# Four moves in a hybrid attention and long-convolution kernel: sample loads, filter negatives, branch matrices, tail stores

## The chip, the cores and the metric

The kernel runs on one core of one Trainium2 chip. A core has five engines that run their own instruction streams in order: TensorE (PE, matmuls and transposes), VectorE (DVE), ScalarE (ACT), GpSimd (POOL) and SyncE (SP, which here only issues transfers). Transfers (DMAs) between the device memory and the on-chip memory are issued by SP, ACT or POOL and carried out by 16 shared DMA engines. The metric is device time in microseconds of one execution; less is better.

## The reference, cut to what matters

Two images of 128 channels and 64x64 positions go through two layers. The first is a windowed attention block with small linear layers. The second flattens each image to 4096 tokens of 128 channels and does a full attention without projections (with a masked diagonal), and then a spectral filter bank: 16 long causal filters `phi`, applied to the sequence and to its sign-alternated copy, mixed by 2x16 matrices of 128x128, plus three short lags. Of four candidate branches one set of weights is formed by a softmax and an argmax.

```python
x = x + conv_block(group_norm(x))                      # layer 0: 7x7 window attention + three linears
t = to_tokens(x)                                       # (2, 4096, 128)
a = layer_norm(t)
sim = a @ a.T / sqrt(128); sim[diagonal] = -1e9
t = t + softmax(sim) @ a                               # layer 1: full attention
u = layer_norm(t)
for i, frac in enumerate((1, 2, 4, 8)):                # layer 1: filters, four branches
    ui = u[:, : T // frac]
    U_plus  = causal_conv(phi, ui)                     # 16 filters
    U_minus = sgn * causal_conv(phi, sgn * ui)
    out_i = einsum(U_plus, sigma**.25, M_plus[i]) + einsum(U_minus, sigma**.25, M_minus[i]) \
          + sum(shift(ui, lag) @ M_u[i][lag] for lag in range(3))
w = one_hot(argmax(y)) - y + y                         # y = softmax(log_weights + gumbel)
out = from_tokens(t + sum(w[i] * pad(out_i)))
```

## The kernel before, in words

All work is float32 on one core. The convolution is done as a transform in blocks: the tokens of each image are transformed by matmuls with a table `tr` into 160 bins (the tensor `us` in device memory), the filters `phi` into the same bins (the tensor `gs`), and the last stage reads both back block by block.

**Stages.** (1) Layer 0 runs in bands of eight image rows through a list of small pieces, written out by hand with due times (`PLAN`); the order on PE, DVE, ACT and POOL is fixed by that list. (2) `attention(0, fill)` runs the full attention of image 0. It goes over pairs (a, c) of eight chunks of 512 tokens; each step makes one score tile (L938), its exponential on ACT (L943) and one product for the keys (L1068). The same weights are needed turned around for the other chunk: four exponential tiles are sent to device memory by ACT (`eb`, L970), read back two steps later by SP into `et` (L977, two buffers), turned in blocks of 32 by DVE at the seventh step (L986), and multiplied by PE from the eighth step on (L996). PE's order is recorded, so if `et` is late PE stands still. (3) `attention(1, fill)` does the same for image 1. (4) A tail finishes the last chunks. (5) The last stage multiplies block by block: `burst` (L1596, copied to `y` at L1601) and `project` (L1615).

**Fillers.** At each step both attentions call `fill()`. It sends waiting stores, and then takes one piece from generators: the `urgent` list (`after`, which divides by the softmax sums, normalises, transforms a finished chunk of 512 tokens into bins and stores them to `us`; and `short_lags`), then the list `steps`. In attention 0 `steps` is: `drain()` (left over pieces of layer 0), `chosen = branch_weights()`, `filters()`, `tokens(1, bank)`. In attention 1 a third list, `slow`, holds `for_ffn()`: it loads the branch matrices (`st`, L1306, 32 loads of 256 KB by POOL), mixes them on DVE (L1328 to L1337) and scales them on ACT (L1342), and last loads the first four blocks for the last stage. It is stepped at every second step: `if turns_[0] % 2: next(slow, None)`. In attention 1 `steps` begins with what attention 0 left in `urgent`.

**Small loads and the POOL queue.** `branch_weights` loads `lw`, `gu` and `sg` on SP (L1253 to L1255); its second piece raises `sg` to a power on POOL (L1259). The filter samples are loaded into `zc` by four DMAs on SP (L906), each of 128x32 runs of eight values (32 bytes); in the built program they stand ahead of the load of `sg`. On POOL, L1259 stands ahead of the pieces that normalise the last chunk of image 0 (`k.pw`, L714 and L715, and `k.z`, L720), which PE transposes next (L202).

**Filters.** `filters()` reads `zc`, transforms it (L1375), accumulates four partial sums in `places` (a region of the tile `cm[1]`), and for each makes sums and differences on POOL (`fb`, L1388) and, for the imaginary parts, the negatives on DVE (`fn`, L1401 and L1402). `fb`, `fn` and the `ub` of `after` (L1169) share one ring of four buffers, tag "ub".

**Stores.** `fresh` puts a store into a list; `stores()` sends it two steps later, on POOL (L1103); `room()` sends more when over three buffers are listed. A ring buffer is free again only when its store has landed. In the tail the sums `ub` are made by DVE, and the stores still go through the list to POOL. The tiles of the last stage (`y` among them) take over memory that the ring has held, so the first copy to `y` waits for the last of the tail's stores.

Of the kernel before, what the change touches and what calls it, by code (L numbers as in the profile page):

```python
# [8 lines left out]
F32 = mybir.dt.float32  # L9
# [5 lines left out]
P = 128  # L15
# [6 lines left out]
KF = 16  # L22
# [80 lines left out]
def kernel(  # L103
# [773 lines left out]
    with ap_:  # L877
# [20 lines left out]

        zc = [tp.tile([P, 2, TH + 1], F32, name="zc"), tt0.rearrange("p (s t) -> p s t", s=2)]
        nc.gpsimd.memset(zc[0][:, :, 0:1], 0.0)  # L900
        pns = {}
        for hh in range(SG // 2):
            for e in range(2):
                at = 1 + (2 * hh + e) * 2 * LG * KF
                pns[hh, e] = zc[0][:, 0, at : at + 2 * LG * KF].rearrange("p (k l f) -> p k l f", k=KF, l=2)
                nc.sync.dma_start(  # L906
                    out=pns[hh, e].rearrange("p k l f -> p (k l) f"),
                    in_=bass.AP(
                        phi_pad.tensor, P - FB + (2 * P * hh + e) * FB, [[2 * FB, P], [PHW, 2 * KF], [1, LG]]
                    ),  # L910
                )

        def attention(b, fill):


# [199 lines left out]
            turns_[1] += 1  # L1115

        def fresh(to, part, by=nc.gpsimd):
            queued_.append((turns_[0], turns_[1], by, to, part))

        def stores_left():  # L1120
            while queued_:
                send_one()


        def after(b, c):

            yield True
            n0 = 4 * c
            par, hf = divmod(c, 4)
            hh, fp = divmod(hf, NFP)  # L1130
            pt = bank()
            for j in range(4):
                nc.tensor.transpose(pt[:, j * P : (j + 1) * P], xa[b][:, (n0 + j) * P : (n0 + j + 1) * P], ident)
            rden = sp.tile([P, 4], F32, tag="rden", name="rden")
            kept_, out_ = tt[b][:, n0 : n0 + 4, :], pt.rearrange("p (j d) -> p j d", d=P)
            nc.vector.reciprocal(rden, out_[:, :, P - 1])
            rest = sp.tile([P, 4], F32, tag="rest", name="rest")
            nc.vector.tensor_reduce(rest, out_[:, :, 0 : P - 1], AX.X, ALU.add)
            for j in range(4):
                nc.vector.scalar_tensor_tensor(  # L1140
                    kept_[:, j, 0 : P - 1], out_[:, j, 0 : P - 1], rden[:, j : j + 1], kept_[:, j, 0 : P - 1],
                    ALU.mult, ALU.add,
                )
            nc.vector.tensor_tensor(rest, rest, rden, ALU.mult)
            nc.vector.tensor_tensor(kept_[:, :, P - 1], kept_[:, :, P - 1], rest, ALU.subtract)
            yield
            z = sp.tile([P, 4, P], F32, tag="z4", name="z4")
            stats = ln_statistics(kept_)
            yield
            yield True  # L1150
            ln_apply(z, kept_, stats)
            yield
            yield True
            pt = bank()
            transposed(pt, z)
            s0 = 1 + 2 * P * hh * FB
            to = zc[b][:, par, s0 : s0 + 2 * P * FB].rearrange("p (c e f) -> p e f c", e=2, f=FB)
            nc.scalar.copy(to[:, :, 2 * fp : 2 * fp + 2], pt.rearrange("p (e f c) -> p e f c", e=2, f=2))
            yield

            def store(pu, n, r0, m, ri):

                for s in range(2):
                    both = sp.tile([P, 512], F32, tag="uo", name="uo", bufs=2)
                    nc.scalar.copy(both[:, 0 : 2 * n], pu[s][:, 0 : 2 * n])  # L1165
                    room()
                    ub = sp.tile([P, 2, 256], F32, tag="ub", name="ub", bufs=4)
                    for sgn, op in enumerate((ALU.add, ALU.subtract)):
                        adder[0].tensor_tensor(ub[:, sgn, 0:n], both[:, 0:n], both[:, n : 2 * n], op)  # L1169
                    to = us[b, par, r0 : r0 + m, :, :, 2 * hh + s, 2 * fp : 2 * fp + 2]  # L1170
                    if ri is not None:
                        fresh(to[:, :, ri].rearrange("k g f d -> k g (f d)"), ub)
                        continue
                    for sgn in range(2):
                        for f in range(2):
                            fresh(to[:, sgn, :, f].rearrange("k i d -> i k d"), ub[64 * f : 64 * f + 64, sgn, 0:P])

            for r0, c0 in row_tiles:
                for ri in range(2):
                    pu = [bank() for _ in range(2)]  # L1180
                    for e in range(2):
                        for s in range(2):
                            rows_ = slice(s * 64, (s + 1) * 64)
                            nc.tensor.matmul(  # L1184
                                pu[s][:, e * 256 : (e + 1) * 256], lhsT=tr[rows_, hh, e, c0 + ri * P : c0 + (ri + 1) * P],
                                rhs=z[rows_, 2 * e : 2 * e + 2, :].rearrange("p f d -> p (f d)"), start=True, stop=True,
                            )
                    store(pu, 256, r0, P, ri)
                    yield
                    if len(crowd_[0]) < 2:  # L1190
                        yield True

            pu = [bank() for _ in range(2)]
            for e in range(2):
                for f in range(2):
                    for s in range(2):
                        rows_ = slice(s * 64, (s + 1) * 64)
                        nc.tensor.matmul(
                            pu[s][f * 64 : (f + 1) * 64, e * P : (e + 1) * P], lhsT=tr[rows_, hh, e, left_col:],
                            rhs=z[rows_, 2 * e + f, :], start=True, stop=True,  # L1200
                        )
            store(pu, P, left_row, 32, None)
            yield
            if len(crowd_[0]) < 2:
                yield True


# [137 lines left out]

        def filters():

            ph = {}
            for (hh, e), pn in pns.items():
                at = (2 * hh + e) * LL  # L1350
# [15 lines left out]
            for r0, c0, parts_, m in everything:  # L1366
                places = cm[1][:, SG * LL : (3 * SG) * LL].rearrange("p (j e c) -> p j e c", j=SG, e=2)
                for j in range(SG):
# [26 lines left out]
                            store(fb[mine], r0, n, ri, s, 1, 1)  # L1395
                    if 1 in parts_:
                        mine = slice(m - n, m)
                        room()
                        fn = sp.tile([P, 2, LL], F32, tag="ub", name="fn", bufs=4)
                        one, two = sums[mine, 0, :], sums[mine, 1, :]  # L1400
                        nc.vector.scalar_tensor_tensor(fn[mine, 0, :], one, -1.0, two, ALU.mult, ALU.subtract)  # L1401
                        nc.vector.tensor_tensor(fn[mine, 1, :], two, one, ALU.subtract)  # L1402
                        store(fn[mine], r0, n, 1, s, 1, 0)
# [8 lines left out]
        def filler(b, steps, kept, slow=()):  # L1412

            urgent, done = [], []
            slow = iter(slow)
            crowd_[0] = urgent

            def fill(c=None):
                if c is not None:
                    done.append(c)  # L1420
                    urgent.append(after(b, c))
                    if len(done) % 4 == 0:
                        lags = short_lags(b, len(done) // 4 - 1)
                        if kept is not None:
                            kept.append(lags)
                            lags = residual_of(lags)
                        urgent.append(lags)
                    return

                stores()  # L1430
                if turns_[0] % 2:
                    next(slow, None)
                for queue in (urgent, steps):
                    while queue:
                        got = next(queue[0], False)
                        if got is None:
                            return
                        if got:
                            break
                        queue.pop(0)  # L1440
                if kept and len(done) == 7:
                    next(kept[0], None)

            return fill, urgent
# [14 lines left out]

        chosen = branch_weights()  # L1460
        next(chosen)
        steps = [drain(), chosen, filters(), tokens(1, bank)]

        kept = []
# [69 lines left out]
        fill, left = filler(1, steps, kept, slow)  # L1534
        attention(1, fill)
        adder[:] = [nc.vector]
        crowd_[0] = [None, None]
        for gen in (*steps, slow):
            for _ in gen:
                pass  # L1540
# [3 lines left out]
        while chains:  # L1544
            for gen in chains[:2]:
                if next(gen, 0) == 0:
                    chains.remove(gen)
                stores()
            next(kept[0], None)
            next(held, None)  # L1550
        stores_left()
        for _ in residuals:
            next(kept[0], None)
            next(held, None)
# [332 lines left out]
```

## Time and profile before

| | us |
|---|---|
| median of three runs (1998.31 to 1998.85) | 1998.82 |
| the profiled execution, its own time | 1999.0 |
| its span in the profile | 1997.2 |
| PE busy | 1906.4 (95%) |
| DVE, ACT, POOL busy | 951.8, 733.0, 749.4 |
| layer 0, and its hand-over to attention 0 | 0 to about 347 |
| attention 0 | about 347 to 767 |
| attention 1 | about 767 to 1172 |
| tail | 1172 to about 1239 |
| last stage | about 1239 to 1997 |

A line of the timeline gives the start, the duration, the engine, the line of the kernel, the operation and how many of it were merged; in square brackets stands the idle time of the engine ahead of it and what ended that. A line of the waits gives the waiting engine and line, what it waited for, and the total, the number and the longest of these waits in microseconds. A line of the table of windows gives the stretch, its length, the busy time of PE, of PE's weight loads, of DVE, ACT and POOL (each with its number of instructions), the granted clock of PE as a share of full speed, the busy share of the DMA engines and GB/s.

### The profile page before, as it was taken

To read this page: it belongs to the slowest core of one execution; us is meant where nothing else is said; L and a number is where in the kernel's file an instruction comes from. 1 tells how busy PE (TensorE), PEld (TensorE's weight loads), DVE (VectorE), ACT (ScalarE), POOL (GpSimd) and SP (SyncE) were. 2 spreads that over 40 slices of the span, in tenths; PEclk is the share of its full clock that TensorE was granted. 3 is DMA by queue.
4 is the path that set the end of the run, shared out by engine and by line. 5 is a ranking of instruction groups with operands and counts; after the bars stand their busy time and mean duration, and the time that the engine had idled before them with its cause. 6 is when DMAs were issued, how large, how long until landed. Compare 5 with 4: busy or idle time off the path is not lost.

```text
span 1997.2 us, 50806 instructions
## 1 busy us (share of the span) xinstructions
PE 1906.4 (95%) x20504; PEld 1350.6 (68%) x20504; DVE 951.8 (48%) x2934; ACT 733.0 (37%) x1718; POOL 749.4 (38%) x1227
## 2 busy tenths in 40 slices
PE   6899998899899999999999998999999999999998
PEld 4677776344344444444444445999998999999987
DVE  5799997354445534454433464333333343333332
ACT  3788986322133333232322313222222222222221
POOL 4366886334542346434332343222222212222211
PEclk8999999899899999999999999999999999999999
DMA  4222222567575543888676413222222223222211
GB/s 156 61 61 59 62 60 49 133 180 221 175 222 163 159 139 116 234 227 249 186 196 192 137 48 86 68 68 66 68 67 54 54 73 85 67 66 69 66 43 44
DMA packets 248185, 226.20 MB, mean 113 GB/s; under 512 B 128495, under 2 KB 202239, under 8 KB 240528
## 3 DMA queue, kind: packets, MB, share of 16 engines
q1 hardware_dynamic: 218482, 125.74, 26.4%
q10 hardware_dynamic: 8126, 58.04, 7.4%
q0 software_dynamic: 21344, 39.18, 6.8%
q8 instruction: 163, 2.67, 0.6%
q14 instruction: 70, 0.57, 0.1%
HBM read 131.40 MB, written 91.25 MB: 111 GB/s over the span
## 4 chain that ended last, share of the span: by engine, by line
PE 77%; DVE 8%; POOL 4%; DMA 4%; issue 2%; SPq 2%; ACT 1%; DVEq 0%; POOLq 0%; ACTq 0%
PE acc L1615 28%; PE own L996 12%; PE bank L938 7%; PE pc L1596 7%; PE other L1068 7%; PE bank L349 2%; PE bank L947 2%; PE bank L559 1%; PE bank L202 1%; PE bank L1184 1%; DVE et L986 1%; DMA et<-eb 1%; DMA us<-ub 1%; ACT p L546 1%; PE bank L1228 1%
## 5 line engine op out<-in xcount | busy, mean ns | idle before, releaser
L1601 DVE COPY y<-pc 128x512 f32<-128x512 f32 x320 | 206.1, 685 | 348.7 <-PE pc L1596 345.7
L1615 PE MATMUL acc<-y,mpl 32*128 32x256 f32 x5120 | 323.7, 379 | 0.8 <-DVE af L1625 0.8
L1601 ACT COPY y<-pc 128x512 f32<-128x512 f32 x320 | 171.9, 589 | 394.8 <-PE pc L1596 381.3
L1615 PE MATMUL acc<-y,mmi 32*128 32x256 f32 x5120 | 315.9, 375 | 0.0
L1615 PEld LDWEIGHTS acc<-y,mpl 32*128 32x128 f32 x5120 | 289.8, 186 | 6.9 <-DVE af L1625 1.3
L1615 PEld LDWEIGHTS acc<-y,mmi 32*128 32x128 f32 x5120 | 291.4, 185 | 2.9
L1626 POOL TENSOR_TENSOR af<-af 128x512 f32<-128x512 f32 x39 | 49.7, 1275 | 573.3 <-DVE af L1625 540.1
L996 PE MATMUL own<-et,tok 128*128 128x512 f32 x448 | 216.6, 606 | 23.8 <-DVE et L986 20.1
L1068 PE MATMUL other<-e,tok 128*128 128x512 f32 x448 | 231.0, 597 | 4.5 <-DVE xa L1077 4.5
L943 ACT ACTIVATE e<-bank 128x512 f32<-128x512 f32 x216 | 129.2, 599 | 276.0 <-PE bank L938 275.9
L938 PE MATMUL bank<-cm 128*128 128x512 f32 x432 | 226.8, 607 | 0.0
L1596 PE MATMUL pc<-ct,ut 32*128 32x256 f32 x2560 | 212.3, 378 | 4.2 <-DVE y L1601 4.2
L1596 PEld LDWEIGHTS pc<-ct,ut 32*128 32x128 f32 x2560 | 172.9, 187 | 10.1 <-DVE y L1601 6.3
L996 PEld LDWEIGHTS own<-et,tok 128*128 128x128 f32 x448 | 84.8, 193 | 135.5 <-issue 103.2
L1169 POOL TENSOR_TENSOR ub<-uo 128x256 f32<-128x256 f32 (+1 forms) x160 | 100.5, 668 | 164.8 <-ACT uo L1165 148.7
L986 DVE STREAM_TRANSPOSE et<-et 128x1024 f32<-128x1024 f32 x108 | 127.7, 1220 | 58.6 <-DMA et<-eb 58.5
L1068 PEld LDWEIGHTS other<-e,tok 128*128 128x128 f32 x448 | 81.3, 191 | 98.8 <-issue 82.7
L1103 POOL DMA_DIRECT2D us<-ub x192 | 131.7, 744 | 18.5 <-DVE ub L1169 9.3
L938 PEld LDWEIGHTS bank<-cm 128*128 128x128 f32 x432 | 76.8, 193 | 74.2 <-issue 67.4
L546 ACT ACTIVATE p<-p,mn 128x196 f32<-128x196 f32 x256 | 114.4, 449 | 14.2 <-DVE mn L536 13.7
L174 POOL TENSOR_TENSOR ln_rs<-ln_rs,mhalf 128x4 f32<-128x4 f32 x24 | 25.0, 1043 | 161.2 <-DVE ln_rs L173 161.2
L1165 ACT COPY uo<-bank 128x512 f32<-128x512 f32 (+1 forms) x96 | 45.4, 518 | 98.2 <-PE bank L1184 58.7
(267 smaller groups left out, 2642.6 us busy)
## 6 DMA issues: line engine op xcount, KB each, us to landing
eb<-e ACTq DMA_DIRECT2D x54, 1024.0 KB
et<-eb SPq DMA_DIRECT2D x216, 256.0 KB
ut<-us SPq DMA_DIRECT2D x156, 128.0 KB
us<-ub POOLq DMA_DIRECT2D x64, 256.0 KB, 3.7
vw<-vd SPq DMA_DIRECT2D x256, 49.0 KB
ct<-gs SPq DMA_DIRECT2D x312, 40.0 KB
ct<-gs SPq DMA_DIRECT2D x312, 32.0 KB
vd<-v SPq DMA_DIRECT2D x128, 32.0 KB
```

Of the source, the lines that this page charges most:

```text
L546: nc.scalar.activation(p, p, AF.Exp, bias=t[name + "mn"][:, h : h + 1], scale=-1.0, accum_out=t["den"][:, u, h : h + 1],)
L938: nc.tensor.matmul(ps.rearrange("p (q t j) -> p q t j", q=4, t=4), lhsT=cm[b][:, n * P : (n + 1) * P], rhs=keys.rearrange("p (t q j) -> p ...
L943: nc.scalar.activation(e, ps.rearrange("p (q r) -> p q r", q=4), AF.Exp, bias=0.0, scale=ASCALE)
L986: in_place(nc.vector.transpose(flat, flat))
L996: nc.tensor.matmul(out_, lhsT=tok[b][:, n, :], rhs=e, start=first, stop=last, skip_group_check=True)
L1068: nc.tensor.matmul(turn(other, "p (q r) -> p q r"), lhsT=tok[b][:, n, :], rhs=es[j], start=(j == 0), stop=(j == 3),)
L1103: by.dma_start(out=to, in_=part)
L1169: adder[0].tensor_tensor(ub[:, sgn, 0:n], both[:, 0:n], both[:, n : 2 * n], op)
L1596: nc.tensor.matmul(pcs[j].rearrange("p (g o c) -> p o g c", g=4, o=2)[:, :, at], lhsT=ut[rows_, par, :], rhs=cv_[rows_], start=True, stop= ...
L1601: (nc.scalar.copy if j % 2 else nc.vector.tensor_copy)(y[:, :, :, 4 * kl + j, :], pcs[j].rearrange("p (g x k) -> p k g x", g=4, k=KF))
L1615: nc.tensor.matmul(acc[j][:, 0:256], lhsT=(mmi if l else mpl)[rows_, k, :], rhs=y[rows_, k, 2 * l : 2 * l + 2].rearrange("p s n x -> p (s ...
L1626: eng.tensor_tensor(af[:, 0:2], af[:, 0:2], af[:, 2:4], ALU.add)
```

## The change

Four edits. The sample loads move from the set-up to just behind the first piece of `branch_weights`, so SP issues `lw`, `gu`, `tr`, `sg` and then the four loads of `zc`. The negatives `fn` get two buffers of their own in the unused end of `cm[1]`, turned by `j % 2`, and no longer call `room()`. `slow` is stepped only once fewer than four generators are left in `steps`; in the built program POOL's first instruction of it (L1517) then stands behind the sixth of the eight small stores of the second of the two chunks of image 0 that attention 1 still has to finish; before, it stood ahead of the stores of the first of them. For the tail the list is emptied first, and `fresh` then issues each store at once on SP.

```diff
-        pns = {}
-        for hh in range(SG // 2):
...
-                nc.sync.dma_start(out=pns[hh, e]..., in_=bass.AP(phi_pad.tensor, ...))
...
         def fresh(to, part, by=nc.gpsimd):
+            if crowd_[0] is None:
+                nc.sync.dma_start(out=to, in_=part)
+                return
             queued_.append((turns_[0], turns_[1], by, to, part))
...
-                    if len(crowd_[0]) < 2:
+                    if crowd_[0] is not None and len(crowd_[0]) < 2:
                         yield True
...
         def filters():
+            negatives = cm[1][:, 3 * SG * LL : (3 * SG + 4) * LL].rearrange("p (a g c) -> p a g c", a=2, g=2)
...
-                        room()
-                        fn = sp.tile([P, 2, LL], F32, tag="ub", name="fn", bufs=4)
+                        fn = negatives[:, j % 2]
...
                 stores()
-                if turns_[0] % 2:
+                if len(steps) < 4 and turns_[0] % 2:
                     next(slow, None)
...
         chosen = branch_weights()
         next(chosen)
+        pns = {}
+        for hh in range(SG // 2):
...
+                nc.sync.dma_start(out=pns[hh, e]..., in_=bass.AP(phi_pad.tensor, ...))
...
         attention(1, fill)
         adder[:] = [nc.vector]
-        crowd_[0] = [None, None]
+        stores_left()
+        crowd_[0] = None
...
             for gen in chains[:2]:
                 if next(gen, 0) == 0:
                     chains.remove(gen)
-                stores()
             next(kept[0], None)
             next(held, None)
-        stores_left()
```

More of the change, by code (lines that the diff above doesn't have):

```diff
@@ L900 @@
         nc.gpsimd.memset(zc[0][:, :, 0:1], 0.0)
-        pns = {}
-        for hh in range(SG // 2):
[L903 to L911, printed above, removed]
         def attention(b, fill):
@@ L1203, in after @@
             yield
-            if len(crowd_[0]) < 2:
+            if crowd_[0] is not None and len(crowd_[0]) < 2:
                 yield True
@@ L1461 @@
         next(chosen)
+        pns = {}
+        for hh in range(SG // 2):
+            for e in range(2):
+                at = 1 + (2 * hh + e) * 2 * LG * KF
+                pns[hh, e] = zc[0][:, 0, at : at + 2 * LG * KF].rearrange("p (k l f) -> p k l f", k=KF, l=2)
+                nc.sync.dma_start(
+                    out=pns[hh, e].rearrange("p k l f -> p (k l) f"),
+                    in_=bass.AP(
+                        phi_pad.tensor, P - FB + (2 * P * hh + e) * FB, [[2 * FB, P], [PHW, 2 * KF], [1, LG]]
+                    ),
+                )
         steps = [drain(), chosen, filters(), tokens(1, bank)]
```

## The prediction

> **What bounds the kernel now.** I read the page's table of engines first, then the table of windows, the waits of PE, and the timelines at the few places where PE stands still.
>
> ```profile
> PE 1906.4 (95%) x20504; PEld 1350.6 (68%) x20504; DVE 951.8 (48%) x2934; ACT 733.0 (37%) x1718; POOL 749.4 (38%) x1227
> ```
>
> PE is the bound; 1997.2 - 1906.4 = 90.8 us of the span it stands still. Only those idle times, and the slow matmuls behind them, can be won. No PE instruction is added, removed or reordered by the edits.
>
> ```profile
> 330.00:370.00 40.00, 26.85 (x213) 16.34 (x214) 15.21 (x72) 11.57 (x28) 23.51 (x30) 0.87 0.41 41
> 480.00:560.00 80.00, 70.50 (x215) 31.35 (x214) 34.97 (x64) 17.02 (x31) 47.25 (x71) 0.94 0.68 199
> 770.00:860.00 90.00, 84.62 (x289) 39.23 (x288) 38.19 (x85) 32.27 (x62) 55.33 (x83) 0.96 0.74 214
> 1172.00:1236.00 64.00, 57.44 (x268) 28.43 (x266) 40.06 (x152) 16.04 (x30) 28.97 (x42) 0.97 0.25 72
> 1236.00:1500.00 264.00, 263.00 (x4832) 261.24 (x4834) 90.76 (x154) 76.12 (x154) 59.48 (x140) 1.00 0.27 68
> ```
>
> PE misses 13.2, 9.5, 5.4 and 6.6 us in four stretches (second column less the PE column), each touched by one edit; the last stage, from 1236, is full and no edit reaches it. In the four the clock column is below 1.00: each long idle time is followed by slow matmuls.
>
> ```profile
> 366.07 0.47 PE L202 MATMUL bank<-ident,tok 128*128 128x128 f32 x1 [7.64 <-POOL tok L720]
> 368.67 1.92 PE L938 MATMUL bank<-cm 128*128 128x512 f32 x2
> 374.27 1.02 PE L938 MATMUL bank<-cm 128*128 128x512 f32 x2
> 523.15 3.70 PE L996 MATMUL own<-et,tok 128*128 128x512 f32 x4 [9.00 <-DVE et L986]
> 808.00 2.90 PE L996 MATMUL own<-et,tok 128*128 128x512 f32 x3 [4.94 <-DVE et L986]
> 1228.63 1.76 PE L1596 MATMUL pc<-ct,ut 32*128 32x256 f32 x14 [3.09 <-DVE y L1601]
> ```
>
> The brackets are the four waits. The second and third lines are the same pair of matmuls just behind the first wait and 5.6 us later.
>
> **The Trainium skill.** "TensorE: Matmul & The Clock Gate", Part 1, says that the array falls to half its clock after an idle window of about 3.4 us and needs about as much busy time to come back. The trace agrees: the six matmuls from 368.67 to 373.42 took 4.75 us where six take 2.58 later, and the four behind the wait of 9.00 took 3.70 where four take 1.88. "DMA: Bandwidth & Descriptors", Specifications, says that pieces under 512 B don't reach full rate; SP's issue of the four sample loads (32-byte pieces) lasted 10.56 us. The same page, "SWDGE vs HWDGE vs iDMA", says that GpSimd computes its descriptors in software and SP doesn't, and gives the first byte as about 1 and 0.6 us. Here POOL pays 0.67 us for a store, SP 0.38 for `ut<-us` and 0.6 for each of four `ct<-gs`.
>
> **Edit 1, sample loads.** What held PE at 366.07 (SP, then POOL):
>
> ```profile
> 343.13 10.56 SPq L906 DMA_DIRECT2D zc<-in_phi_pad_dram  x4
> 353.74 2.50 SPq L1255 DMA_DIRECT2D sg<-in_sigma_dram  x1
> 349.56 1.49 POOL L676 TENSOR_SCALAR y<-y 128x512 f32<-128x512 f32 x1
> 359.16 2.93 POOL L1259 TENSOR_TENSOR sg<-sg,quarter 128x16 f32<-128x16 f32 x1 [8.11 <-DMA sg<-in_sigma_dram]
> ```
>
> POOL was free at 349.56 + 1.49 = 351.05, and waited 8.11 us for `sg`, which stood behind the sample loads. In the new order SP issues `sg` at 343.13; its transfer took 5.35 us behind those loads, so it lands by about 348.5, before POOL comes. The power, two `m_u` issues, L714 and L715 and the first `tok` tile take 366.07 - 359.16 = 6.91 us, so the first tile is there at 357.96 and PE, which ends its earlier work at 366.07 - 7.64 = 358.43, doesn't wait. The last of four tiles comes 8.11 us earlier: 8.1 us gained, and 4.75 - 2.58 = 2.2 of slow clock: **10**. What is late next: the four `zc` loads, by one issue (0.4 to 2.5 us); they end about 356 on SP, the `et` loads behind them are first issued after 360, and DVE first reads `zc` at 455. Bounds 7 (slow clock stays) and 10.5.
>
> **Edit 2, negatives.** At 523:
>
> ```profile
> 505.20 0.42 DVE L1401 SCALAR_TENSOR_TENSOR fn<-cm 128x256 f32<-128x256 f32 x1 [11.45 <-POOL fb L1388]
> 520.05 0.43 DVE L1401 SCALAR_TENSOR_TENSOR fn<-cm 128x256 f32<-128x256 f32 x1 [12.90 <-DMA gs<-fb]
> 520.73 2.36 DVE L986 STREAM_TRANSPOSE et<-et 128x1024 f32<-128x1024 f32 x2
> ```
>
> DVE stood 12.90 us for a buffer of the ring, and the turn that PE needed was behind it in DVE's order. With own buffers the first `fn` needs only ACT's copy (500.62 + 0.58), the second follows at about 504 to 507, and the turn ends near 510, if `et` is there: SP issued that load at 495.26. PE wants it at 523.15 - 9.00 = 514.15. So 9.0 us go, and 3.70 - 1.88 = 1.8 of slow clock: 10.8. The new wait: the third `fn` takes the first one's buffer and waits for its store. `fb` of the second sum waits for stores issued up to 501, runs near 508, the stores of the first pair follow to 512, and `gs<-fn` lands in 4.2 us: 516. Behind that `fn` on DVE are `xa` (PE's next L1068 needs it near 520) and the next diagonal tile; up to 3 us could come back. I take **10**; bounds 5 and 11. The eight `fn` fewer in the ring also let `fb` and `ub` run earlier; I count nothing.
>
> **Edit 3, matrices.** POOL issued `inv` at 772.28 and seven loads of 256 KB by 808.82, while the stretch from 782 to 806 moved 246 GB/s at 0.84 busy.
>
> ```profile
> 805.53 2.37 DVE L986 STREAM_TRANSPOSE et<-et 128x1024 f32<-128x1024 f32 x2 [10.91 <-DMA et<-eb]
> ```
>
> The turn waited for `et`, whose transfer from 794.23 took 11.10 us, behind an `eb` of 6.58. In the new order POOL's first issue stands where 824.5 is now, 52.7 us later. Between 782 and 806 six loads, 1.6 MB of 5.9, are gone (27%): `et` should land some 4 to 5 us earlier, against a wait of 4.94, with 1.3 us of slow clock behind it. The same loads then share the steps from 824 to about 1090 instead of 772 to 1036: DVE's 40 mixing operations of about 0.7 us, ACT's 32 scalings and POOL's 20 block loads move with them; all had room (DVE 48%), and the block loads, moved from 1002-1037 to about 1055-1090, are needed at 1224. But 1040 to 1100 already moved 192 GB/s, and 942 shows two late turns at 262 GB/s just before. Gain 6 at best; I take **4**; bounds -4 and +8 (the 2.70 us wait at 945 could go too).
>
> **Edit 4, tail stores.** (POOL, then DVE:)
>
> ```profile
> 1218.68 5.86 POOL L1103 DMA_DIRECT2D us<-ub  x9 [1.45 <-DVE ub L1169]
> 1227.89 1.29 DVE L1601 COPY y<-pc 128x512 f32<-128x512 f32 x2 [2.25 <-DMA us<-ub]
> ```
>
> The last store is issued by 1223.86 and lands at 1227.41, and only then may `y` be written. Before it DVE waited 1.33 + 0.39 + 1.54 + 2.15 + 0.17 = 5.6 us for ring buffers, which held ACT and then PE (1.21 + 0.49 for `uo`, 1.35 for L1244). With SP at 0.4 to 0.6 us an issue, right behind each `ub`, 24 stores take 10 to 14 us from 1204: the last `ub` is done near 1215.5 instead of 1219.4, the last store lands near 1221. PE comes 1.70 us earlier to L1228, doesn't wait 1.35, and at the second burst waits the 0.76 that the third shows instead of 3.09: 1.70 + 1.35 + 2.33 = 5.4, and about 1 of slow clock. **6**; bounds 2 (SP's stores land no sooner) and 8. Behind the stores on SP are only the fifth block's loads, first issued at 1225.73 before.
>
> **Sum.** 10 + 10 + 4 + 6 = 30 of the profiled execution's 1999.0, span 1997.2 and 1.8 around it: 1969.0. It lies 0.2 above the median of 1998.82; I forecast 1969. All low ends: 10 gained, 1989; all high ends: 37.5, 1961.
>
> **The rivals.** *Half of it comes back at the negatives.* For: the ring of two is shorter than the ring of four, and stores landed in up to 6.97 us there. Against: the turn stands ahead of the third `fn`. Then 5 instead of 10: 1974 to 1977. *The matrices are a mere shift.* For: the same 8.4 MB in as many steps; nothing won at 808 or lost again near 1090: 1973 to 1977. *Slower, by the moved matrices.* `st`, `us`, `eb` and `et` share the DMA engines; with the loads 52.7 us later, the far pairs from 824 to 1090 (27 in the some 405 us of an attention, one each 15 us, so 18) run with `et` late. At 945 such a pair cost 2.70; 18 x 2.7 = 49, less the other 26: 2022. It decides from 1.5 us a pair. Against: the old stretch held the same loads and lost 9.5 in all. *The change does not do what it says*: `sg` still lands after 359 because `tr` (640 KB, issued just ahead) fills the queue: edit 1 gives 0 to 3 and the time is 1976 to 1979.
>
> **How the numbers follow.** All four as summed, 1963 to 1973: 0.52. Half back at the negatives: 0.15. Matrices a mere shift: 0.18. No gain from `sg`: 0.05. Two of these together, 1980 to 1990: 0.05. About no change: 0.02; slower: 0.03. Within 0.2% means 1994.8 to 2002.8, about what a measurement of this kernel can tell. So faster 0.95, same 0.02, slower 0.03. The range 1960 to 1985 leaves out a part of two together, no change and slower at one end, and a time below all high ends (1961) at the other.
>
> **What would show it.** Edit 1: no wait of PE for L720 over 1 us and POOL's L1259 starting near 351. Edit 2: no DVE wait over 5 us for `fn`, no PE wait near 513. Edit 3: the first `st` of 256 KB some 15 steps into attention 1, and PE's wait for `et` behind 40 us of it under 1. Edit 4: `us<-ub` on SP in the tail, the second burst's wait under 1.5. It is wrong if PE waits for `et` grow by over 5 us between 860 and 1170, or if new waits for `fn` take the place of the 9.00.

## The result, and the profile after

The changed kernel took 1975.9 us (median of six runs, 1969.95 to 1980.67) against 1998.93 for the kernel before (six runs, 1998.31 to 2001.74): a ratio of 0.988, with a 95% interval of 0.986 to 0.990. That is 23 us less, where 30 were forecast. The profiled execution is the shortest of the six, 1969.95 us with a span of 1968.2; against the profiled execution before (span 1997.2) it gained 29.0. So the profile stands close to the forecast of 1969.0, and the median 6 us above the profile. Both facts want an explanation.

The table of engines on the page of the changed kernel:

```profile
PE 1897.2 (96%) x20504; PEld 1346.5 (68%) x20504; DVE 950.2 (48%) x2934; ACT 732.6 (37%) x1718; POOL 725.6 (37%) x1193
```

PE has the same 20504 instructions and is busy for 9.2 us less (fewer matmuls at the slow clock); it stands still for 1968.2 - 1897.2 = 71.0 us, where it was 90.8. POOL's 34 instructions fewer are the tail's stores. The windows of the changed kernel, at the three first stretches of before (at the same times, so their contents have moved by up to 27 us), and the tail from its start to the third burst, after and then before:

```profile
330.00:370.00 40.00, 34.41 (x237) 19.67 (x235) 19.45 (x88) 17.05 (x39) 24.18 (x31) 0.96 0.51 79
480.00:560.00 80.00, 77.41 (x241) 34.86 (x241) 40.22 (x82) 21.44 (x38) 48.01 (x74) 1.00 0.77 222
770.00:860.00 90.00, 88.81 (x287) 41.43 (x286) 32.98 (x61) 27.94 (x50) 43.26 (x66) 1.00 0.84 234
1137.70:1207.30 69.60, 63.53 (x282) 31.30 (x282) 42.58 (x158) 16.65 (x31) 8.03 (x11) 0.98 0.22 67
```

```profile
1166.40:1236.60 70.20, 63.01 (x280) 31.00 (x280) 42.49 (x158) 16.64 (x31) 31.02 (x46) 0.98 0.24 68
```

PE now misses 5.6, 2.6, 1.2 and, in the tail, 6.1 us. The first three were 13.2, 9.5 and 5.4 and have shrunk; the tail, 7.2 before, has hardly. The granted clock (the column behind POOL) says the same: 0.96, 1.00 and 1.00, and still under 1 in the tail.

The same places in the timeline of the changed kernel, PE:

```profile
358.88 0.33 PE L202 MATMUL bank<-ident,tok 128*128 128x128 f32 x1 [0.45 <-POOL tok L720]
359.82 1.02 PE L926 MATMUL bank<-cm 128*128 128x512 f32 x2
509.07 1.12 PE L1056 MATMUL other<-e,tok 128*128 128x512 f32 x2 [1.74 <-DVE xa L1065]
784.04 1.96 PE L984 MATMUL own<-et,tok 128*128 128x512 f32 x4 [1.01 <-POOL ub L1160]
1194.26 4.51 PE L1219 MATMUL acc<-tt,mu 128*128 128x512 f32 x6 [2.80 <-DVE xa L1235]
1200.72 1.89 PE L1597 MATMUL pc<-ct,ut 32*128 32x256 f32 x16 [0.88 <-DVE y L1602]
```

Line numbers have moved with the edits: L926, L984, L1056, L1219 and L1597 here are L938, L996, L1068, L1228 and L1596 of before. The wait of 7.64 has become 0.45, and the first score matmuls behind it take 1.02 us a pair at once, instead of 1.92. The 9.00 and the 4.94 are gone; 1.74 and 1.01 stand where they were. At the second burst 3.09 has become 0.88. But the line above it is new: 2.80 us for `xa`, where the same wait had been 1.35 us, and six matmuls behind it at 4.51 us. The same instruction before:

```profile
1221.66 2.81 PE L1228 MATMUL acc<-tt,mu 128*128 128x512 f32 x6 [1.35 <-DVE xa L1244]
```

Where the time went can be read off by finding the same PE instruction in both timelines and subtracting the start times:

| same PE instruction (before, after) | start before | start after | ahead by |
|---|---|---|---|
| first score tile of attention 0 | 346.46 | 345.86 | 0.6 |
| attention 0 | 469.34 | 458.32 | 11.0 |
| attention 0, after the filters' pairs | 559.63 | 540.12 | 19.5 |
| end of attention 0 | 764.18 | 744.16 | 20.0 |
| attention 1 | 891.75 | 865.14 | 26.6 |
| attention 1 | 969.83 | 940.51 | 29.3 |
| start of the tail | 1166.43 | 1137.66 | 28.8 |
| third burst | 1236.63 | 1207.22 | 29.4 |

In this execution edit 1 brought 10.4, edit 2 about 8.5 to 9, edit 3 8.8, and edit 4, the tail, 0.6.

### The profile page after: what moved, and what is told of

It reads as the page before. It is cut to its first block, busy times and chain, and to the rows that moved or that the text cites. A ratio compares the mean times of both kernels' runs of the same rounds, so it can differ in the third digit from the quotient of the medians.

```text
span 1968.2 us, 50791 instructions
## 1 busy us (share of the span) xinstructions
PE 1897.2 (96%) x20504; PEld 1346.5 (68%) x20504; DVE 950.2 (48%) x2934; ACT 732.6 (37%) x1718; POOL 725.6 (37%) x1193
## 4 chain that ended last, share of the span: by engine, by line
PE 82%; DVE 8%; POOL 4%; DMA 2%; issue 1%; ACT 1%; SPq 1%; ACTq 0%; DVEq 0%; POOLq 0%
PE acc L1616 28%; PE own L984 12%; PE bank L926 8%; PE other L1056 8%; PE pc L1597 7%; PE bank L349 2%; PE bank L935 2%; PE bank L559 2%; PE bank L1219 2%; PE bank L1175 2%; PE bank L202 2%; DVE et L974 1%; PE bank L523 1%; PE pc L1655 1%; PE po L581 1%
## 5 line engine op out<-in xcount | busy, mean ns | idle before, releaser
L1602 ACT COPY y<-pc 128x512 f32<-128x512 f32 x320 | 171.8, 589 | 393.3 <-PE pc L1597 388.1
L1056 PE MATMUL other<-e,tok 128*128 128x512 f32 x448 | 230.1, 595 | 6.8 <-DVE xa L1065 6.8
L926 PE MATMUL bank<-cm 128*128 128x512 f32 x432 | 223.6, 599 | 0.0
L984 PE MATMUL own<-et,tok 128*128 128x512 f32 x448 | 212.1, 596 | 9.1 <-DVE et L974 4.7
L1597 PE MATMUL pc<-ct,ut 32*128 32x256 f32 x2560 | 210.1, 377 | 2.0 <-DVE y L1602 2.0
L1597 PEld LDWEIGHTS pc<-ct,ut 32*128 32x128 f32 x2560 | 171.5, 186 | 8.3 <-DVE y L1602 3.8
L984 PEld LDWEIGHTS own<-et,tok 128*128 128x128 f32 x448 | 83.2, 190 | 118.3 <-issue 93.7
L974 DVE STREAM_TRANSPOSE et<-et 128x1024 f32<-128x1024 f32 x108 | 127.7, 1220 | 57.6 <-DMA et<-eb 57.6
L1056 PEld LDWEIGHTS other<-e,tok 128*128 128x128 f32 x448 | 81.0, 190 | 100.5 <-issue 82.4
L926 PEld LDWEIGHTS bank<-cm 128*128 128x128 f32 x432 | 75.7, 190 | 72.8 <-issue 66.5
L1091 POOL DMA_DIRECT2D us<-ub x158 | 107.8, 723 | 11.5 <-DMA us<-ub 8.5
```

Of the source, the lines that this page charges most:

```text
L926: nc.tensor.matmul(ps.rearrange("p (q t j) -> p q t j", q=4, t=4), lhsT=cm[b][:, n * P : (n + 1) * P], rhs=keys.rearrange("p (t q j) -> p ...
L974: in_place(nc.vector.transpose(flat, flat))
L984: nc.tensor.matmul(out_, lhsT=tok[b][:, n, :], rhs=e, start=first, stop=last, skip_group_check=True)
L1056: nc.tensor.matmul(turn(other, "p (q r) -> p q r"), lhsT=tok[b][:, n, :], rhs=es[j], start=(j == 0), stop=(j == 3),)
L1091: by.dma_start(out=to, in_=part)
L1597: nc.tensor.matmul(pcs[j].rearrange("p (g o c) -> p o g c", g=4, o=2)[:, :, at], lhsT=ut[rows_, par, :], rhs=cv_[rows_], start=True, stop= ...
```

## The experiments

Questions were open on three things. Do the four edits act apart, and what is each worth? Why does the tail stay as long as it was, although no store of it goes through POOL any more? And what separates a run of the changed kernel at 1970 from one at 1980? The first theory for the last was that the moved matrices do it. Runs of one group below shared a chip and the runs of the kernel before.

### Each edit alone

Each kernel is the kernel before with the hunk of one edit.

**Edit 1 alone:** the four sample loads behind `lw`, `gu` and `sg`.

```diff
-                nc.sync.dma_start(out=pns[hh, e]..., in_=bass.AP(phi_pad.tensor, ...))   # in the set-up
+                nc.sync.dma_start(out=pns[hh, e]..., in_=bass.AP(phi_pad.tensor, ...))   # behind next(chosen)
```

> The kernel before with edit 1 alone (sample loads behind the load of sg). Theory A (the profile of the changed kernel read stall by stall): PE's wait for L720 and the slow clock behind it go and nothing comes back: 10 us less than before, about 1989, runs within 1.5 us of each other. Theory B (an earlier start only makes PE wait later, since et is bound by the transfers): under 5 us less, with longer PE waits for et (L986's line) before 560.

Measured: 1985.99 us against 1998.66 (ratio 0.9944, 0.9922 to 0.9966), 12.7 less by the medians; the interval, 6.8 to 15.6 us, takes in the 10 forecast. The wait for L720 is gone (0.5 at most). The wait of 9 us of edit 2 is untouched, PE in the timeline of this kernel:

```profile
512.07 3.37 PE L984 MATMUL own<-et,tok 128*128 128x512 f32 x4 [8.98 <-DVE et L974]
```

So edit 1 doesn't take the gain of edit 2 with it.

**Edit 2 alone:** buffers of their own for the negatives.

```diff
-                        room()
-                        fn = sp.tile([P, 2, LL], F32, tag="ub", name="fn", bufs=4)
+                        fn = negatives[:, j % 2]
```

> The kernel before with edit 2 alone (negatives in a place of their own). Theory A: the 9.00 us wait and its slow clock go, a new wait of about 1.7 us for xa stands 12 us behind: 8 to 9 us less than before, about 1990, runs within 1.5 us of each other. Theory B (the 8.5 us belong to the two edits together, since with edit 1 alone the wait would have moved anyway): under 5 us less.

Measured: 1987.98 us (0.9939, 0.9916 to 0.9963), 10.7 less. The 9.00 is gone, a wait of 0.87 us for `xa` stands behind it, and 7.18 us for L720 remain. The runs of edits 1 and 2 alone lie up to 10 and 17 us apart, where 1.5 was expected.

**Edit 3 alone:** the matrices later.

```diff
-                if turns_[0] % 2:
+                if len(steps) < 4 and turns_[0] % 2:
```

> The kernel before with edit 3 alone (branch matrices from step 15). Theory A: it is this edit that makes the changed kernel's times vary by 11 us: between 2 and 9 us less than before, 1990 to 1997, and runs spread over 5 us or more. Theory B (the spread comes from the stores or the negatives): runs within 2 us of each other, at 1990 to 1992, and the spread shows in one of the other kernels.

Measured: 1994.84 us (0.9983, 0.9971 to 0.9995), 3.8 less. PE in its timeline:

```profile
801.61 1.96 PE L996 MATMUL own<-et,tok 128*128 128x512 f32 x4 [1.18 <-POOL ub L1169]
936.88 3.62 PE L996 MATMUL own<-et,tok 128*128 128x512 f32 x4 [3.55 <-DVE et L986]
```

The late turn near 800 is gone, as forecast (4.94 before, now 1.18 for something else), but a late turn near 937 is there in full. With the matrices moved it is 3.55 us, where the first profile of before had 2.70 near 945. On this chip the kernel before itself ran from 1990.89 to 2010.37 in 42 runs. The spread of single runs is therefore not the work of edit 3, nor of any edit, and that theory falls.

**Edit 4 alone:** the tail's stores at once on SP.

```diff
+            if crowd_[0] is None:
+                nc.sync.dma_start(out=to, in_=part)
+                return
```

> The kernel before with edit 4 alone (tail's stores at once by SP). Theory A: SP issues the small stores one after the other at 0.5 to 0.7 us, so DVE's wait for ring buffers stays and PE's wait moves from y (L1601) to xa (L1244): 0 to 1.5 us less than before, 1997.5 to 1999. Theory B (the forecast of 6 holds and was given back elsewhere in the changed kernel): 5 to 7 us less, about 1993.

Measured: 1999.32 us (1.0003, 0.9988 to 1.0019): no gain. The medians of the four alone add to 12.7 + 10.7 + 3.8 - 0.7 = 26.5 us. PE at the tail:

```profile
1222.18 2.81 PE L1231 MATMUL acc<-tt,mu 128*128 128x512 f32 x6 [2.85 <-DVE xa L1247]
1228.68 2.83 PE L1598 MATMUL pc<-ct,ut 32*128 32x256 f32 x16 [2.61 <-DVE y L1603]
```

The wait for `y` was expected to move to `xa`. It stayed, at 2.61 after 3.09, and the one for `xa` grew from 1.35 to 2.85 beside it.

### One edit taken back, and why the tail stayed

The next group ran on another chip, where the kernel before had a median of 1998.85 us and the changed kernel, run again, had this to meet:

> The changed kernel once more, as the base for the other runs of this call. If the four edits add up (12.7 + 10.7 + 3.8 - 0.7 = 26.5 by their medians alone), the median is 1971 to 1977. If edits share a gain, it is above 1980.

Measured: 1978.11 us (1972.69 to 1980.7; 0.9897, 0.9876 to 0.9918), 20.7 less than before. That lies between the two expectations, so these medians don't tell whether the edits share a gain. Its profiled execution has a span of 1974.2, 6.0 longer than that of the first. Where they come from is taken up below.

**Without edit 4:** the other three.

```diff
-            if crowd_[0] is None:
-                nc.sync.dma_start(out=to, in_=part)
-                return
```

> The changed kernel with the tail's stores back on POOL through the list. Theory A (edit 4 is worth nothing, since the wait for the ring only changes its place): within 2 us of the changed kernel; PE waits near 3 us for y instead of 2.8 for L1235's xa. Theory B (edit 4 pays only together with the others): 4 to 6 us slower.

Measured: 1976.06 us (0.989, 0.9871 to 0.9909), the same as with it. So no gain of edit 4 shows beside the others either. The waits expected in its profile did not come: PE waits 0.8 us for `y`, not near 3, and 2.1 for `xa`.

The trace of the changed kernel says why. Here are SP's last 22 stores of the tail, in two rows, DVE's waits for ring buffers in the tail before and after (in all, times, longest), and part of the chain of waits through the tail (start, length, engine, what):

```profile
1178.97 9.55 SPq L1107 DMA_DIRECT2D us<-ub  x13
1191.02 5.12 SPq L1107 DMA_DIRECT2D us<-ub  x9
```

```profile
DVE ub L1169 <- DMA us<-ub: 5.6, 5, 2.1
DVE ub L1160 <- DMA us<-ub: 5.7, 3, 2.9
```

```profile
1187.26 4.20 DMA us<-ub
...
1191.54 0.49 DVE ub L1160 x2
1192.04 2.08 DVE xa L1235 x8
1194.12 0.14 issue
1194.26 4.51 PE acc L1219 x6
```

SP issued 22 stores in 17.2 us: thirteen close behind one another, then nine, and 2.5 us between the rows in which it had nothing to send, because DVE itself stood without a buffer. The store in the chain takes 4.20 us until it has landed and its ring buffer is free. DVE stood 0.57 + 2.92 + 2.24 = 5.7 us for ring buffers, as long as before (5.6). Behind the ring in DVE's order stand the last `ub` and then `xa` (L1235), which PE's L1219 needs. The last store started 1195.6 - 1137.66 = 57.9 us into the tail; before, on POOL, it was at 1223.9 - 1166.43 = 57.5. The issuing engine was changed and the pace stayed. What remains is whether the ring's four buffers or the one queue sets the pace.

**Eight buffers in the tail:** `ub` of the tail in free room of `cm[1]`, the stores still on SP.

```diff
-                    ub = sp.tile([P, 2, 256], F32, tag="ub", name="ub", bufs=4)
+                    if crowd_[0] is None:
+                        at_ = (turns_[1] % 8) * 512
+                        ub = cm[1][:, at_ : at_ + 512].rearrange("p (a c) -> p a c", a=2)
+                    else:
+                        ub = sp.tile([P, 2, 256], F32, tag="ub", name="ub", bufs=4)
```

> The changed kernel with eight buffers for ub in the tail (in cm[1], which is free then) instead of the ring of four. Theory A (four buffers whose stores land 3 to 4 us after an issue that takes its turn are what holds DVE, ACT and PE in the tail): DVE's waits for us<-ub go, PE's 2.80 us for xa and 0.45 + 0.90 for uo go: 3 to 5 us less than the changed kernel. Theory B (SP's 24 issues of 0.5 us or more in a row are the limit): the wait moves to y (L1602) behind the last store, and the time is within 1.5 us of the changed kernel.

Measured: 1976.74 us (0.9897, 0.9874 to 0.992): nothing gained. DVE's waits for the ring are gone and the wait for `xa` is down to 1.31, but PE and DVE in its timeline show

```profile
1203.85 2.67 PE L1601 MATMUL pc<-ct,ut 32*128 32x256 f32 x16 [5.59 <-DVE y L1606]
1203.11 1.29 DVE L1606 COPY y<-pc 128x512 f32<-128x512 f32 x2 [4.70 <-DMA ct<-gs]
```

and SP still issues its last store at 1197.6. The ring's wait has only turned into the next one, 5.59 us for `y`. What ended last before the copy to `y` was not a store but a load of the last stage, `ct`, which SP issues behind the row of stores. So the single queue is a second limit right behind the first.

**Eight buffers and two issuers:** as the last, and the small stores on POOL, the large on SP.

```diff
-                nc.sync.dma_start(out=to, in_=part)
+                (nc.gpsimd if part.shape[0] == 64 else nc.sync).dma_start(out=to, in_=part)
```

> The eight tail buffers, with the small stores issued by POOL and the large ones by SP. Theory A (SP's 24 issues in a row are what is left in the tail: y waited 5.59 us behind them): two issuers end the stores some 5 us earlier, the wait for y falls under 1.5 us, the tail is 4 to 6 us shorter than in the changed kernel and the median 1971 to 1975. Theory B (the stores' landing is the limit, whoever issues them): the wait for y stays above 4 us and the median is within 1.5 us of the changed kernel's 1978.

Measured, on a third chip (before: 1999.43): 1973.82 us (0.9871, 0.9853 to 0.989). PE in its timeline:

```profile
1202.27 2.81 PE L1223 MATMUL acc<-tt,mu 128*128 128x512 f32 x6 [1.31 <-DVE xa L1239]
1206.97 1.73 PE L1601 MATMUL pc<-ct,ut 32*128 32x256 f32 x16 [0.81 <-DVE y L1606]
```

Both waits are short at last. From the start of the tail to the third burst it takes 64.8 us, where the kernel before needs 70.2, the changed kernel 69.6 and 69.3 in its two profiles, and the one with eight buffers on SP alone 72.0. That is 5.4 us less than before, near the 6 forecast for edit 4. More buffers alone did not bring it; more buffers and a second issuer did. A second issuer with the ring of four was not run, so whether the buffers are needed beside it is not shown. Of the whole time the run can't show so little: its interval overlaps that of the changed kernel.

### The turn near 920

Windows of the changed kernel, its first profile and then the one run again:

```profile
880.00:905.00 25.00, 25.00 (x78) 11.31 (x79) 8.67 (x10) 7.00 (x13) 16.43 (x25) 1.00 0.97 276
905.00:930.00 25.00, 23.58 (x63) 10.69 (x62) 10.96 (x18) 7.06 (x17) 2.24 (x3) 1.00 0.75 205
```

```profile
880.00:905.00 25.00, 25.00 (x79) 11.40 (x79) 8.73 (x10) 7.01 (x13) 16.16 (x25) 1.00 0.96 272
905.00:930.00 25.00, 20.36 (x48) 9.21 (x47) 11.05 (x18) 5.42 (x15) 2.00 (x4) 0.86 0.72 168
```

From 880 to 905 the two can't be told apart: PE is full and the DMA engines are busy for 0.97 and 0.96 of the time. The loss comes only afterwards, when PE reaches a group whose `et` is late. In the run again:

```profile
920.50 3.78 PE L984 MATMUL own<-et,tok 128*128 128x512 f32 x4 [4.64 <-DVE et L974]
```

In the first profile the turns there cost 0.57 and 0.85. Attention 1 is 6.7 us longer in the run again (400.2 against 393.5), and most of that stands here: 4.64 - 1.42 = 3.2 is wait and 3.78 - 1.98 = 1.8 slow clock. In that stretch the matrices (256 KB each), the small stores of a finished chunk, `eb` and `et` all move. The loads of this `et` (SP), the matrix loads beside them (POOL) and the turn itself (DVE), in the first profile and then in the run again:

```profile
903.64 1.73 SPq L965 DMA_DIRECT2D et<-eb  x4
903.46 0.77 POOL L1297 DMA_DIRECT2D st<-in_m_plus_dram  x1 [0.48 <-issue]
913.92 2.36 DVE L974 STREAM_TRANSPOSE et<-et 128x1024 f32<-128x1024 f32 x2
```

```profile
903.66 1.74 SPq L965 DMA_DIRECT2D et<-eb  x4
903.73 1.55 POOL L1297 DMA_DIRECT2D st<-in_m_plus_dram  x2 [0.90 <-DMA us<-ub]
918.07 2.37 DVE L974 STREAM_TRANSPOSE et<-et 128x1024 f32<-128x1024 f32 x2 [3.98 <-DMA et<-eb]
```

The `et` loads are issued at the same times. In the run again POOL had waited for a store, and two matrix loads instead of one stand beside them (the one ahead of it in the first profile was issued at 902.17). That is one pair of profiles; it suggests a cause and doesn't show it.

**Without edit 3:** the matrices early again, the others kept.

```diff
-                if len(steps) < 4 and turns_[0] % 2:
+                if turns_[0] % 2:
```

> The changed kernel with the branch matrices from the first step again. Theory A (the gain of edit 3 is the wait for et near 785): a PE wait of 5 to 6 us for et with slow matmuls behind it is back there, and the time is 4 to 7 us above the changed kernel. Theory B (with the earlier edits the loads meet the exchange of eb and et at other steps, so it is a mere shift): within 2 us.

Measured: 1979.22 us (0.9903, 0.9884 to 0.9922), only 1.1 above the changed kernel on the same chip, within the intervals. Its profile (an execution of 1984.07) has both late turns, 5.54 at 791 and 5.74 at 930. So edit 3 takes the wait near 790 away, as forecast, but not the one near 930, and in the medians of the full kernel its worth can't be told from nothing, against 3.8 alone.

**Not while stores wait:** once fewer than four generators are left, `slow` is stepped at every step at which no store is listed.

```diff
-                if len(steps) < 4 and turns_[0] % 2:
+                if len(steps) < 4 and not queued_:
```

> The changed kernel, but the branch matrices are stepped at every step at which no store waits in the list, instead of at every second step (same 32 loads, ended some 20 steps earlier). Theory A (PE's wait for et near 920 comes from loads and stores issued together, at 0.96 of the DMA engines busy from 880 to 905): that wait goes from 4.6 to under 1.5 us, and the median falls by 3 to 6 us, to 1972 to 1975. Theory B (the exchange of eb and et and the stores alone are enough, or the denser loads make others late): the sum of PE's waits for et stays at 8 us or grows, and the median is at 1976 or above.

Measured: 1971.95 us (0.9863, 0.9845 to 0.988). PE waits 0.83 us near 921, and 2.0 for the transposed `et` (L974) over all of attention 1, where the run again had 5.8 and the first profile 2.6.

**Two of five steps:** a thinner stream of loads, without regard to the stores.

```diff
-                if len(steps) < 4 and turns_[0] % 2:
+                if len(steps) < 4 and turns_[0] % 5 in (0, 2):
```

> The changed kernel with the branch matrices stepped at two of five steps instead of one of two (the same loads, a fifth thinner, ended 24 steps later). Theory A (what counts is which loads meet the stores): the wait for et near 920 stays within 2 us of 4.6 or moves, median within 3 us of 1978. Theory B (the mean rate counts): waits for et fall by a third or more everywhere, median 1973 to 1975.

Measured: 1972.31 us (0.9864, 0.9845 to 0.9883), with a wait of 0.57 near 922. To thin the loads looks as good as to keep them clear of the stores. Whether the collision or the mean rate makes `et` late isn't told apart by these. Their intervals still touch that of the changed kernel, which was not run on this chip, and its first profile had waits as short near 920 (0.57 and 0.85) without either, so by these runs alone neither is shown to help.

**The two findings together:** eight buffers, small stores on POOL, and `slow` only while no store waits.

```diff
+                (nc.gpsimd if part.shape[0] == 64 else nc.sync).dma_start(out=to, in_=part)
...
+                if len(steps) < 4 and not queued_:
```

> Eight tail buffers with two issuers, and matrices stepped only where no store waits. If both theories A hold the gains add, as they lie 250 us apart: 1966 to 1971. If only the tail's holds: 1971 to 1975; if neither: 1976 or above.

Measured: 1966.81 us (1965.1 to 1969.12), a ratio of 0.9839 (0.9822 to 0.9856) to the kernel before. This interval lies apart from those of the changed kernel (0.986 to 0.990 and 0.9876 to 0.9918): it is faster than both kernels, 32.6 us below the one before. In its profile the tail takes 64.7 us, and PE near 918 and at the second burst shows

```profile
917.89 1.98 PE L984 MATMUL own<-et,tok 128*128 128x512 f32 x4 [1.67 <-DVE et L974]
1195.94 1.73 PE L1601 MATMUL pc<-ct,ut 32*128 32x256 f32 x16 [0.96 <-DVE y L1606]
```

and from 880 to 905 the DMA engines are busy for 0.84 of the time at 245 GB/s, instead of 0.96 or 0.97.

**The stages of all fourteen profiles.** The four PE instructions that bound the stages in the table further up (first score tile of attention 0, end of attention 0, start of the tail, third burst) give each stage's length in every profile kept here:

| stage | kernels | us |
|---|---|---|
| attention 0 | without edits 1 and 2 (three) | 417.0 to 418.0 |
| | edit 1 alone; edit 2 alone | 406.9; 407.7 |
| | with both (nine) | 397.2 to 402.6 |
| attention 1 | without edit 3 (five) | 399.1 to 405.1 |
| | with edit 3 (six) | 393.5 to 401.2 |
| | with edit 3 and the loads kept clear of the stores or thinned (three) | 393.3 to 394.9 |
| tail | stores on POOL (five) | 68.1 to 70.2 |
| | stores on SP, four buffers (six) | 68.4 to 71.5 |
| | eight buffers, SP alone; with two issuers | 72.0; 64.7 and 64.8 |

Edits 1 and 2 take 10 to 11 us each off attention 0 when alone and 15 to 20 together, so there they act apart, or nearly. All five profiles without edit 3 have a turn late by 4.9 to 5.9 us near 800, and none of the nine with it waits over 2.0 us there. The later turn, between 916 and 945, is late by 0.6 to 5.7 us without edit 3 and by 0.6 to 4.6 with it, and so hides most of what edit 3 gains (4.1 us between the two averages) in a single run. With the loads kept clear or thinned it stays at 0.6 to 1.7. Three profiles, one of each kernel, point that way and don't prove it. So of the difference between a run at 1970 and one at 1980, up to 7.7 us lie in attention 1, and up to 3.6 in when attention 0 starts.

## Why the prediction was right, and which term was wrong

The direction was right, and 1975.9 lies within the range of 1960 to 1985. That the profiled execution met 1969.0 within 1 us is luck: there edit 3 gave 8.8 instead of 4, and edit 4 0.6 instead of 6. By its own steps:

**Edit 1 held, step by step.** Forecast were 8.1 us of wait and 2.2 of slow clock, 10 in all; the alignment shows 10.4, the run alone 12.7 by the medians and 10.8 in attention 0 of its profile. SP and POOL in the changed kernel:

```profile
342.54 0.50 SPq L1246 DMA_DIRECT2D sg<-in_sigma_dram  x1
343.08 10.18 SPq L1458 DMA_DIRECT2D zc<-in_phi_pad_dram  x4
350.42 2.92 POOL L1250 TENSOR_TENSOR sg<-sg,quarter 128x16 f32<-128x16 f32 x1
```

SP issues `sg` ahead of the sample loads, and POOL takes it up at 350.42 (forecast: near 351) without a wait. The rival that `tr`, ahead of it, would still hold `sg` until 359 is out.

**Edit 2 held, with its new wait.** 10 were forecast from a bound of 5 to 11; it brought 8.5 to 9 in the alignment, and alone 10.7 by the medians and 10.0 in attention 0 of its profile. The third negative waits for the store of the first, as forecast. DVE:

```profile
494.26 2.36 DVE L974 STREAM_TRANSPOSE et<-et 128x1024 f32<-128x1024 f32 x2
507.66 0.42 DVE L1392 SCALAR_TENSOR_TENSOR cm<-cm 128x256 f32<-128x256 f32 x1 [5.74 <-DMA gs<-cm]
```

The turn that PE needed stands ahead of it now (494.26), so the 5.74 us fall on DVE alone but for `xa`, which is late by 1.74 for PE. The prediction had put up to 3 us on exactly that. Only its sign "no DVE wait over 5 us for `fn`" failed: the wait is 5.74 us, but most of it had slack before PE needed `xa`. The rival "half of it comes back" would have left 5, and the interval of edit 2 alone is 7.4 to 16.8, so it is out.

**Edit 3: the mechanism held, the size is not settled.** 4 was forecast, within -4 to 8. Alone it gave 3.8, in the first profile 8.8, in the full kernel by medians about 1, and between the averages of the profiles 4.1. The first matrix load of 256 KB is issued at 799.09 (782.25 before, with 20 us gained by then). The forecast that PE's wait for `et` would keep under 1 us in the 40 us behind it was true of both profiles of the changed kernel (0.18 at most). The late turn lies further on: 0.57 and 0.85 in the first profile, 4.64 in the run again. The prediction had named this place ("942 shows two late turns at 262 GB/s just before") but gave it no spread from run to run. The rival of a slower kernel, late `et` at each of 18 far pairs, is out: PE's waits for `et` between 860 and 1170 were 3.8 + 1.4 before and 2.6 + 1.4 or 5.8 + 1.4 after.

**Edit 4 is the term that failed: 6 forecast, nothing measured** (0.7 slower alone, 0.6 gained in the alignment, no difference when taken back). The step that failed is "24 stores take 10 to 14 us from 1204: the last `ub` is done near 1215.5". It took SP's time for one issue (0.4 to 0.6 us; the median was 0.52, right) and let each store go right behind its `ub`. But a `ub` needs a ring buffer, and a buffer is free only when its store has been issued, behind the others on the one queue, and has landed, 2.9 and 4.2 us after the issue for two stores in the chain. The price of an issue had been compared; the loop through ring and landing had not. 22 stores took 17.2 us, where POOL's last 22 had taken 16.5. The last `ub` was done 54.4 us into the tail, where 49.1 was forecast (1215.5 - 1166.43) and 53.0 measured before. DVE's ring waits of 5.6 us, listed in the prediction, were taken to shrink with the issue and stayed at 5.7, so the time saved at `y` (3.09 to 0.88) came back at `xa` (1.35 to 2.80), and the slow clock that had stood behind `y` (six matmuls in 4.04 us) now stood behind `xa` (4.51). The low end of 2 should have been 0. The Trainium skill, "DMA: Bandwidth & Descriptors", section "Issuing engines are not separate DMA queues", says that issuing on several engines at once saves only the sequencer's time to start a transfer, "which is usually small relative to the DMA itself". For one store the runs agree: 0.52 us of issue on SP and 0.66 to 0.73 on POOL, beside 2.6 to 4.0 us to landing for POOL's stores before. In a row it is not small: the 22 issues fill 9.55 + 5.12 = 14.7 us of SP, and with eight buffers a second issuer shortened the tail.

So the missing 7 us of the medians (30 less 23) are the 6 of edit 4, and the rest lies in edit 3, whose worth changes with the run. Slow clock behind waits was sized well: behind 4.64 us four matmuls took 3.78 us, without a wait 1.88, and behind waits of 1.0 to 1.7 us 1.96 to 1.98. "TensorE: Matmul & The Clock Gate", Part 1, puts the fall to half clock at an idle window of about 3.4 us. Shorter waits were followed by slow matmuls here too: four took 3.28 us behind 2.58 (eight buffers), and six 4.51 behind 2.80, while six behind 2.85 in edit 4 alone took 2.81. So these runs give no sharp limit at 3.4 us.

What stays open: why one execution meets a late `et` at 920 and another doesn't, whether rate or collision with the stores decides it, and whether a second issuer would do without more buffers. A part of the spread lies elsewhere: the first score tile of attention 0, which no edit touches, starts between 344.57 and 348.15 in the profiles of all these kernels.

## What to carry to other kernels

Where a stage ends in many small stores from a short ring, price the whole loop (buffer, issue behind the others, landing), not the issue: here the ring, the one queue and the landing stood in a row; more buffers alone released nothing, and more buffers with a second issuer 5 us. For a stalled PE, look at what stands in the feeding engine's order ahead of the instruction that PE needs: two edits that only removed a wait standing there gave 19 of the 29 us of the profiled execution. And don't take the worth of a moved transfer from one profile: beside stretches in which the DMA engines are 0.96 busy it was 9 us in one execution and 1 in the medians.

## What was not expected of the hardware

The DMA engines can be busy for 0.96 to 0.97 of a stretch of 25 us (272 to 276 GB/s) while PE loses nothing in it. What follows some 15 us later is one late turn, and the share doesn't tell how late: 0.97 was followed by 0.57 and 0.85 us in one profile and by 2.58 in another (eight buffers), and 0.87 by 4.43 (eight buffers and two issuers). And the kernel before, which agreed within 3.4 us in its first six runs, spread over 20 us (1990.89 to 2010.37) in 42 runs on another chip, so that six runs that agree don't say how wide the next ones will lie.
